# Context turned on VectorE in three pieces, the keys' turn moved one step later, and another order of the last copies and table loads, in a cross-attention kernel

## The chip, the cores and the metric

The kernel runs on one core of a Trainium2 chip. The metric is device time in microseconds (us). Before the change three runs took 446.92, 447.15 and 447.34 us; the median is 447.15 us. The profile comes from one further execution.

## The reference, cut to what matters

Eight batches, each with 112 query rows of 320 channels and a context of 375 rows of 512: 371 text tokens and 4 prompt tokens. There are 20 heads of 16 channels, all in float32.

```python
q   = heads(hidden_states @ W_q)
k_t = heads(text_ehs @ W_k);  v_t = heads(text_ehs @ W_v)
probs_t  = softmax(einsum('bhsd,bhtd->bhst', q, k_t) * attn_scale)
text_out = einsum('bhst,bhtd->bhsd', probs_t, v_t)
k_ip = heads(ip_ehs @ W_k_ip);  v_ip = heads(ip_ehs @ W_v_ip)
qsem = l2norm(einsum('bhst,bte->bhse', probs_t, text_ehs))
sem  = einsum('bhse,bne->bhsn', qsem, l2norm(ip_ehs))
fused = einsum('bhsd,bhnd->bhsn', q, k_ip) * attn_scale + 0.5 * sem
ip_out = einsum('bhsn,bhnd->bhsd', softmax(fused) * spatial_mask, v_ip)
out = (text_out + ip_out) @ W_out + b_out + hidden_states
```

The length of `qsem` is had without forming it: with the context's own product `G = ctx ctx^T`, its square is `p G p^T` for each row of probabilities `p`. So one wide product of `p` gives the value sums, the dots with the prompts and `p G` at once.

## The kernel before, in words

**Per batch, the context is turned first.** `ct` (128 x 3 x 512) holds 375 rows, 128 to a chunk. `transposed_context(b)` turns each chunk with four TensorE transposes (L357) into a bank of PSUM, and ScalarE copies it (L367) into `ctxT`, with the 512 features on the partitions (4 blocks `e` of 128) and the tokens along the row. From `ctxT` come `gram(b)` (L415), `values(b)` (L486) and `keys(b)` (L453). All three sum over the 512 features; so the order in which features lie on `e` and on the partitions doesn't matter as long as the weights are laid out in the same order (`load_embed`, L114). The last 64 channels of the keys come as extra columns of `values`, are put in `k3`, and are turned by three TensorE transposes (L444): this is the keys' last chunk.

**Heads go in five groups of four.** A step is a pair (b, g). For each step:

- `scores` (L592, PSUM pool `ps_sc` of two banks) and `probabilities` run two steps ahead (`LEAD`): VectorE takes the maximum (L605), ScalarE the exponential (L609), and a DMA from SP's queue copies `p` into `xg` (L614). `ps_sc` also serves other products that ask for a `spare` bank; the rest take one of the two banks of `ps_mm`.
- `transposed` turns a group's `xg` on VectorE (L622), one step ahead, after the third of the twelve parts of the running product.
- `multiplied` is the product (L641): 12 parts of 4 heads, into four banks of PSUM (`ps_qd`, four in all). The next step's product needs those banks again, so they must have been read.
- `value_sums` (ScalarE, L654) and `reduced` (VectorE, L687, four times) read them; after the last read the banks are free.
- `between(b, g)` puts the next batch's preparation on TensorE in this place, while the banks are read: for g = 0 the gram, for 1 two thirds of the values, for 2 the rest of the values and the first chunk of keys, for 3 the second chunk, the turn of the third (L444) and the transposes of the finished batch's attention (L837, `finish`), for 4 the context of batch b + 2 (L357), the output product (L849) and a chunk of queries (L305).

**The order of the work** on TensorE, VectorE and SP is written out by hand and so, after the prologue, is ScalarE's; GpSimd (POOL) is placed by the scheduler until the last batch, and by hand there. SP's one queue issues nearly all DMAs in order, each `xg` copy among them. `load_next(b + 2)` issues the four DMAs of a context at the end of step (b, 0), four steps ahead of its turn at (b, 4).

**The end** (batch 7) has no next batch. After the last product, `finish(b, (0, 16))` treats sixteen heads, `last_heads` the last four, and `finish(6)`, called `before`, is still to be completed. Each needs a square root, then an exponential, and ScalarE loads a table (`preload_act_table`) for each change of function. The statements from `value_sums(b, g)` on (L1180 to L1199) set this order.

Of the kernel before, what the change touches and what calls it, by code (L numbers as in the profile page):

```python
# [8 lines left out]
F32 = mybir.dt.float32  # L9
AF = mybir.ActivationFunctionType  # L10
# [10 lines left out]
def kernel(  # L21
# [15 lines left out]
    P = 128  # L37
# [20 lines left out]

    GROUP = 4
# [54 lines left out]
    def load_embed(eng, t, w):  # L114
        eng.dma_start(t[:, :, :C], w.rearrange("(e p) f -> p e f", p=P))
# [7 lines left out]

    def load_ctx(b):
        ct = io.tile([P, NT, E], F32, tag="ct", name=f"ct_{b}")
        for c in range(NT):
            rows = min(P, T - c * P)
            some = rows - rows % 16
            nc.sync.dma_start(ct[:some, c, :], ehs[b, c * P : c * P + some, :])
            if some < rows:  # L130
                nc.sync.dma_start(ct[some:rows, c, :], ehs[b, c * P + some : c * P + rows, :])
        return ct
# [82 lines left out]
    def normalised_prompts():  # L215

        sq = work.tile([N, E], F32, tag="ipn", name="ipsq", bufs=1)
        ss = small.tile([N, 1], F32, tag="ipss", name="ipss", bufs=1)
        nc.vector.tensor_tensor_reduce(
            out=sq, in0=ip_sb, in1=ip_sb, scale=1.0, scalar=0.0, op0=ALU.mult, op1=ALU.add,  # L220
            accum_out=ss,
        )
        nc.vector.tensor_scalar_max(ss, ss, EPS * EPS)
        rn = small.tile([N, 1], F32, tag="iprn", name="iprn", bufs=1)
        nc.scalar.activation(rn, ss, AF.Sqrt)
        nc.vector.reciprocal(rn, rn)

        ipn = work.tile([N, E], F32, tag="ipn", name="ipn", bufs=1)
        nc.vector.tensor_scalar(ipn, ip_sb, rn, 0.5, op0=ALU.mult, op1=ALU.mult)
        yield  # L230

        for src, dst, n in ((ipn, ipnT, "n"), (ip_sb, ipT, "r")):
            ps = bank(f"ps_ipT{n}")
            for e in range(NE):
                nc.tensor.transpose(
                    ps[:, e * N : (e + 1) * N], src[:, e * P : (e + 1) * P], ident[:N, :N]
                )
            nc.vector.tensor_copy(
                dst, ps[:, : NE * N].rearrange("p (e n) -> p e n", n=N)
            )  # L240
        yield
# [86 lines left out]
    def begin(b):  # L328
        s = st[b] = dict(ct=loaded.pop(b))
        s["ctxT"] = work.tile([P, NE, TP], F32, tag="ctxT", name=f"ctxT_{b}")  # L330
        nc.gpsimd.memset(s["ctxT"][:, :, T:], 0.0)

        s["kT"] = work.tile([P, NC, T], F32, tag="kT", name=f"kT_{b}")
        s["vext"] = work.tile([P, NT, C + REST], F32, tag="vext", name=f"vext_{b}", bufs=1)
# [14 lines left out]
    def transposed_context(b):  # L349
        begin(b)  # L350
        s = st[b]
        ct, ctxT = s["ct"], s["ctxT"]
        for c in range(NT):
            rows = min(P, TT - c * P)
            ps = bank(f"ps_c_{b}_{c}", spare=b > 1 and c > 0)
            for e in range(NE):
                nc.tensor.transpose(  # L357
                    ps[:, e * P : e * P + rows],
                    ct[:rows, c, e * P : (e + 1) * P],
                    ident[:rows, :rows],  # L360
                )
# [72 lines left out]
    def keys(b):  # L434
# [3 lines left out]
        for i in range(NC):  # L438
            ps = bank(f"ps_k_{b}_{i}")
# [39 lines left out]
    def values(b):  # L479
        s = st[b]  # L480
        ctxT, vext = s["ctxT"], s["vext"]
# [222 lines left out]
    def finish(b, heads=(0, H), bd=None):  # L704
# [69 lines left out]
        if bd is not None:  # L774
# [9 lines left out]
            for i in range(i0, i1):  # L784
# [10 lines left out]
                )  # L795
            aT = work.tile([P, NC, S], F32, tag="aT", name=f"aT_{b}_{h0}")
# [84 lines left out]
    def last_heads(b):  # L881
# [9 lines left out]
        def over_ip(t):  # L891
# [16 lines left out]
        nc.scalar.preload_act_table(AF.Exp)  # L908
        yield
# [8 lines left out]
        nc.scalar.activation(ex, fu, AF.Exp)  # L918
        nc.vector.tensor_reduce(sx, ex, AX.X, ALU.add)
        nc.vector.reciprocal(rx, sx)  # L920
        nc.vector.scalar_tensor_tensor(w, ex, sm_sb, over_ip(rx), ALU.mult, ALU.mult)
        yield

        ps = bank(f"ps_a_{b}_{h0}")
        nc.tensor.transpose(ps[:, :S], attn[:, FULL * P :], ident[:S, :S])
        aT = work.tile([P, NC, S], F32, tag="aT", name=f"aT_{b}_{h0}")
        nc.scalar.copy(aT[:, FULL, :], ps[:, :S])
        nc.tensor.matmul(
            s["o"][:S, :C], aT[:, FULL, :], wo_sb[:, FULL, :], start=False, stop=False
        )  # L930
# [6 lines left out]
        nc.scalar.copy(wT[:k], ps[:k, :S])  # L937
        nc.tensor.matmul(s["o"][:S, :C], wT[:k], s["bw"], start=False, stop=True)
# [14 lines left out]
    LEAD = 2  # L953
# [11 lines left out]
    def between(b, g):  # L965
# [26 lines left out]
        if g == 3:  # L992
            if new:
                run(("k", nb), None, 1)
            for bs in first if b > 0 else ():
                run(("q", bs[0]), lambda: project_queries(bs), 3)
            if b == 0:
                run(("t", b), lambda: prompt_logits(b))
            if nb < B - 1:
                run(("k", nb), None, 1)  # L1000
            if b > 0 and new:
                run(("f", b - 1), None)
            for bs in rest:
                run(("q", bs[0]), None)
        if g == 4:
            if nb + 1 < B:
                run(("c", nb + 1), lambda: transposed_context(nb + 1))
            if b > 0 and new:
                run(("f", b - 1), None, 2)
            if nb + 1 < B:  # L1010
                run(("c", nb + 1), None, 2)
# [51 lines left out]
    for n, (b, g) in enumerate(steps[:-NG]):  # L1063
# [27 lines left out]
        if g == 0:  # L1091
            load_next(b + 2)
        elif g == 1:
# [91 lines left out]
    run(before, None)  # L1185
    next(late)
# [3 lines left out]
    nc.scalar.preload_act_table(AF.Sqrt)  # L1190
    run(before, None)
    reduced(b, g, 1)
    next(first)
    last = last_heads(b)
    next(last)
# [47 lines left out]
```

## Time and profile before

| | |
|---|---|
| median of three runs | 447.15 us (446.92 to 447.34) |
| the profiled execution | 447.37 us, span 445.6 us |
| TensorE matmuls busy | 433.7 us (97%) |
| VectorE busy | 306.9 us (69%) |
| ScalarE busy | 197.0 us (44%) |
| GpSimd busy | 111.1 us (25%) |
| packets of SP's DMA queue | 51530, 53.4% of 16 DMA engines' span |
| granted TensorE clock | 0.997 |

The span runs from the first instruction to the last. Busy time counts overlapping instructions once. "PE" is TensorE, "PEld" its weight loads, "DVE" VectorE, "ACT" ScalarE, "POOL" GpSimd, "SPq" the instructions by which SP issues DMAs. An entry "A <- B" of waiting says that A stood idle until B had ended. The chain of waits is followed back from the last instruction to what released it, step by step.

### The profile page before, as it was taken

To read this page: it belongs to the slowest core of one execution; us is meant where nothing else is said; L and a number is where in the kernel's file an instruction comes from. 1 tells how busy PE (TensorE), PEld (TensorE's weight loads), DVE (VectorE), ACT (ScalarE), POOL (GpSimd) and SP (SyncE) were. 2 spreads that over 40 slices of the span, in tenths; PEclk is the share of its full clock that TensorE was granted. 3 is DMA by queue.
4 is the path that set the end of the run, shared out by engine and by line. 5 is a ranking of instruction groups with operands and counts; after the bars stand their busy time and mean duration, and the time that the engine had idled before them with its cause. 6 is when DMAs were issued, how large, how long until landed. Compare 5 with 4: busy or idle time off the path is not lost.

```text
span 445.6 us, 13074 instructions
## 1 busy us (share of the span) xinstructions
PE 433.7 (97%) x5096; PEld 335.3 (75%) x5096; DVE 306.9 (69%) x646; ACT 197.0 (44%) x667; POOL 111.1 (25%) x270
## 2 busy tenths in 40 slices
PE   8998999999999999999999999999999999999895
PEld 8756767888778877788777787788777887787783
DVE  3047366786687767686687866776687867878783
ACT  2254232335345353343534453333535454436773
POOL 4302201011150111511142120612124111527340
PEclk9999999999999999999999999999999999999998
DMA  8769954544645466555646366455556436563300
GB/s 241 188 165 259 202 144 138 142 141 138 171 122 135 144 171 164 130 134 143 164 119 166 113 179 165 120 143 152 155 166 145 140 86 180 134 144 105 92 2 26
DMA packets 52031, 64.26 MB, mean 144 GB/s; under 512 B 18354, under 2 KB 44130, under 8 KB 51970
## 3 DMA queue, kind: packets, MB, share of 16 engines
q1 hardware_dynamic: 51530, 62.88, 53.4%
q8 instruction: 40, 0.66, 0.7%
q10 hardware_dynamic: 440, 0.56, 0.4%
q14 instruction: 21, 0.17, 0.1%
HBM read 18.72 MB, written 5.32 MB: 54 GB/s over the span
## 4 chain that ended last, share of the span: by engine, by line
PE 91%; ACT 3%; DMA 2%; DVE 1%; POOL 1%; SPq 0%; issue 0%; POOLq 0%; DVEq 0%; ACTq 0%
PE ps_qd L641 42%; PE ps_v L486 14%; PE ps_k L453 9%; PE ps_g L415 8%; PE ps_s L592 4%; PE ps_q L305 3%; PE ps_c L357 2%; PE ps_o L849 2%; ACT p L609 1%; PE ps_g L387 1%; DMA vr<-vd 1%; DMA xg<-p 1%; DVE xgT L622 1%; PE ps_k L469 1%; DMA ct<-in_ctx_dram 1%; POOL shared L676 1%
## 5 line engine op out<-in xcount | busy, mean ns | idle before, releaser
L641 PE MATMUL ps_qd<-u,xgT 32*112 32x104 f32 (+11 forms) x3840 | 217.9, 351 | 3.1 <-DVE xgT L622 1.2
L641 PEld LDWEIGHTS ps_qd<-u,xgT 32*112 32x112 f32 x3840 | 185.7, 172 | 36.2 <-issue 9.8
L605 DVE TENSOR_REDUCE nmx<-ps_s 112x1 f32<-112x371 f32 x160 | 77.5, 529 | 72.8 <-PE ps_s L592 72.8
L622 DVE STREAM_TRANSPOSE xgT<-xg 128x1536 f32<-128x1536 f32 x40 | 119.0, 2975 | 7.8 <-DMA xg<-p 7.8
L609 ACT ACTIVATE p<-ps_s,nmx 112x371 f32<-112x371 f32 x160 | 87.0, 583 | 80.6 <-DVE nmx L605 58.4
L687 DVE CUSTOM_DVE_ANT_0 junk<-ps_qd,p 112x371 f32<-112x371 f32 x148 | 80.2, 542 | 15.7 <-ACT pvs L654 0.2
L559 POOL COPY u<-vr 128x64 f32<-128x64 f32 x120 | 25.8, 237 | 162.4 <-PE ps_qd L641 105.6
L592 PE MATMUL ps_s<-kT,qm 32*112 32x375 f32 (+1 forms) x320 | 64.0, 481 | 0.4 <-ACT p L609 0.4
L486 PE MATMUL ps_v<-wv_sb,ctxT 128*128 128x384 f32 (+1 forms) x192 | 63.5, 480 | 0.0
L486 PEld LDWEIGHTS ps_v<-wv_sb,ctxT 128*128 128x128 f32 x192 | 35.2, 190 | 19.7
L453 PE MATMUL ps_k<-ctxT,wk_sb 128*128 128x371 f32 x136 | 45.9, 482 | 0.0
L654 ACT COPY pvs<-ps_qd 112x21 f32<-112x21 f32 x150 | 15.9, 190 | 63.1 <-PE ps_qd L641 63.1
L415 PE MATMUL ps_g<-ctxT 128*128 128x375 f32 (+2 forms) x168 | 37.4, 379 | 0.0
L453 PEld LDWEIGHTS ps_k<-ctxT,wk_sb 128*128 128x128 f32 x136 | 25.1, 190 | 15.3 <-issue 0.5
L415 PEld LDWEIGHTS ps_g<-ctxT 128*128 128x128 f32 x168 | 28.1, 190 | 8.4
L592 PEld LDWEIGHTS ps_s<-kT,qm 32*112 32x112 f32 x320 | 25.6, 170 | 5.8 <-ACT kT L460 2.0
L314 DVE TENSOR_SCALAR qm<-ps_q,emask 128x224 f32<-128x224 f32 (+1 forms) x25 | 9.2, 400 | 21.8 <-PE ps_q L305 21.8
L611 ACT COPY ipl<-ps_s 112x4 f32<-112x4 f32 x140 | 23.6, 169 | 0.0
L493 ACT COPY vext<-ps_v 128x384 f32<-128x384 f32 (+1 forms) x24 | 11.2, 467 | 24.3 <-PE ps_v L486 24.3
L460 ACT COPY kT<-ps_k 128x371 f32<-128x371 f32 x17 | 8.0, 469 | 26.0 <-PE ps_k L453 26.0
L403 ACT ACTIVATE ug<-ps_g 128x375 f32<-128x375 f32 (+2 forms) x24 | 9.0, 377 | 23.0 <-PE ps_g L415 18.7
L824 POOL TENSOR_TENSOR wv<-vip,w 112x1280 f32<-112x1280 f32 x6 | 14.8, 2461 | 14.6 <-DVE w L770 14.6
(158 smaller groups left out, 333.1 us busy)
## 6 DMA issues: line engine op xcount, KB each, us to landing
xg<-p SPq DMA_DIRECT2D x160, 162.3 KB
u<-ug SPq DMA_DIRECT2D x128, 99.0 KB
ct<-in_ctx_dram SPq DMA_DIRECT2D x16, 256.0 KB
vr<-vd SPq DMA_DIRECT2D x32, 120.0 KB
vip<-vipd SPq DMA_DIRECT2D x6, 560.0 KB
vd<-vext SPq DMA_DIRECT2D x7, 320.0 KB
ct<-in_ctx_dram SPq DMA_DIRECT2D x8, 224.0 KB
vd<-vext SPq DMA_DIRECT2D x7, 160.0 KB
```

The costliest lines, as they stand in the source:

```text
L415: nc.tensor.matmul(ps[:, : T - t0], ctxT[:, e, t0 : t0 + P], ctxT[:, e, t0:T], start=(e == 0), stop=(e == NE - 1),)
L453: nc.tensor.matmul(ps[:, :TT], wk_sb[:, e, i * P : (i + 1) * P], s["ctxT"][:, e, :TT], start=(e == 0), stop=(e == NE - 1),)
L486: nc.tensor.matmul(ps[:, :w], ctxT[:, e, c * P : (c + 1) * P], wv_sb[:, e, :w], start=(e == 0), stop=(e == NE - 1),)
L559: nc.gpsimd.tensor_copy(region(b, c)[:, :, UV - c * P :], s["vr"][:, c * QN : (c + 1) * QN, g, :])
L592: nc.tensor.matmul(ps[:S, :w], qm[a * RG : (a + 1) * RG, i, r, j * S : (j + 1) * S], s["kT"][a * RG : (a + 1) * RG, i, :w], start=True, st ...
L605: nc.vector.tensor_reduce(nmx, ps[:S, :TT], AX.X, ALU.max, negate=True)
L609: nc.scalar.activation(p, ps[:S, :TT], AF.Exp, bias=nmx)
L611: nc.scalar.copy(s["ipl"][:, groups[g][a], :], ps[:S, TT:T])
L622: nc.vector.transpose(xT.rearrange("p j (k q) -> p q j k", q=QN), xg.rearrange("p q (j k) -> p q j k", k=RG),)
L641: nc.tensor.matmul(banks[a][:S, j * RG : UW], xT[a * RG : (a + 1) * RG, j, :S], region(b, c)[a * RG : (a + 1) * RG, q, q * RG :], start=(j ...
L654: nc.scalar.copy(s["pvs"][:, h, :], ps[:S, TT:UW])
L687: nc.vector.tensor_tensor_reduce(out=junk, in0=ps[:S, :TT], in1=s["p", g][:, a, :], scale=1.0, scalar=0.0, op0=ALU.mult, op1=ALU.add, accu ...
```

## The change

Batches 0 and 1 are turned as before. For batches 2 to 7:

- the context is loaded in another layout: each 32 tokens x 128 features go to a block of 32 partitions (`v`, 12 columns of 128 features), by eight DMAs in place of four: four of 32 x 11 runs of 128 floats, and four of 19 rows of 128 floats for the rest. A memset on GpSimd clears the last column first;
- three VectorE transposes (32 x 32 blocks, 128 x 512 elements each) write `ctxT` in place of twelve TensorE transposes and three ScalarE copies. They stand one each in `between` for g = 0, 1 and 2 (for batch 0: 1, 2, 3), so that the turn is finished at (b, 2) and no longer at (b, 4); the load is issued at the end of step (b - 1, 4), one step ahead of its first use. Batch 2's is issued at the end of step (0, 0), as before;
- since a partition now holds features `4 p + e`, the weights that multiply `ctxT` are loaded in that order too, and the transposes that remain on TensorE read every fourth feature (`chunk`).

In `between`, the turn of the keys' third chunk (L444) goes from g = 3 to g = 4, into a bank of `ps_sc`; the transposes of the finished batch's attention stand right behind the keys' second chunk. At the end, the table of the square root is loaded ahead of the copies of `aT`, the products of the outputs come after the transposes of the last heads' attention, and the last heads' square root and exponential come ahead of the copy of the sixteen heads' `aT`.

```diff
     def load_embed(eng, t, w):
-        eng.dma_start(t[:, :, :C], w.rearrange("(e p) f -> p e f", p=P))
+        eng.dma_start(t[:, :, :C], w.rearrange("(p e) f -> p e f", e=NE))
+    def chunk(t, e):
+        return t.rearrange("t (p e) -> t e p", e=NE)[:, e, :]
     def load_ctx(b):
         ct = io.tile([P, NT, E], F32, tag="ct", name=f"ct_{b}")
+        if b >= LEAD:
+            v = ct.rearrange("p c e -> p (c e)").rearrange("p (j f) -> p j f", f=P)
+            full = TT // RG
+            nc.gpsimd.memset(v[:, full, :], 0.0)
+            for a in range(QN):
+                nc.sync.dma_start(
+                    v[a * RG : (a + 1) * RG, :full, :],
+                    ehs[b, : full * RG, a * P : (a + 1) * P].rearrange("(j i) f -> i j f", i=RG),
+                )
+            for a in range(QN):
+                nc.sync.dma_start(
+                    v[a * RG : a * RG + TT - full * RG, full, :],
+                    ehs[b, full * RG : TT, a * P : (a + 1) * P],
+                )
+            return v
...
     def begin(b):
-        nc.gpsimd.memset(s["ctxT"][:, :, T:], 0.0)
+        if b < LEAD:
+            nc.gpsimd.memset(s["ctxT"][:, :, T:], 0.0)
...
     def transposed_context(b):
+        if b >= LEAD:
+            for c in range(NT):
+                some = slice(c * QN, (c + 1) * QN)
+                nc.vector.transpose(
+                    ctxT[:, :, c * P : (c + 1) * P].rearrange("p e (j i) -> p j e i", i=RG),
+                    ct[:, some, :].rearrange("p j (k e) -> p j e k", e=NE),
+                )
+                yield
+            return
...
     def keys(b):
-            ps = bank(f"ps_k_{b}_{i}")
+            ps = bank(f"ps_k_{b}_{i}", spare=0 < b < B - 1 and i == FULL)
...
     def between(b, g):
         if g == 3:
             if new:
                 run(("k", nb), None, 1)
+            if b > 0 and new:
+                run(("f", b - 1), None)
...
-        if g == 4:
-            if nb + 1 < B:
-                run(("c", nb + 1), lambda: transposed_context(nb + 1))
-            if b > 0 and new:
-                run(("f", b - 1), None, 2)
-            if nb + 1 < B:
-                run(("c", nb + 1), None, 2)
+        if 0 <= g - (b == 0) < NT and nb + 1 < B:
+            run(("c", nb + 1), lambda: transposed_context(nb + 1))
+        if g == 4:
+            if b > 0 and new:
+                run(("f", b - 1), None, 2)
+            if nb < B - 1:
+                run(("k", nb), None, 1)
...
-        if g == 0:
+        if n == 0:
             load_next(b + 2)
-        elif g == 1:
+        if g == NG - 1:
+            load_next(b + 3)
+        if g == 1:
...
     late = projected_prompts(bd[:, 1])
     run(before, None)
     next(late)
-    run(before, None)
-    next(late)
+    nc.scalar.preload_act_table(AF.Sqrt)
+    run(before, None, 2)
     reduced(b, g, 0, 1)
     next(first)
     next(first)
-    nc.scalar.preload_act_table(AF.Sqrt)
-    run(before, None)
+    next(late)
     reduced(b, g, 1)
     next(first)
     last = last_heads(b)
     next(last)
+    run(before, None)
+    next(last)
+    next(first)
     next(last)
     next(first)
     next(last)
```

`finish` has one more `yield` between the transposes and the copy of `aT`, `last_heads` issues its transpose (L925) right behind the square root and its product (L928) behind the transposed weights' copy, and `vext` is allocated in `values` and no longer in `begin`.

## The prediction

> **What bounds the kernel now.** I read the busy times first, then the chain of waits, then the timeline around one step of kind g = 4, then VectorE's own timeline, and last the end.
>
> ```profile
> PE 433.7 (97%) x5096; PEld 335.3 (75%) x5096; DVE 306.9 (69%) x646; ACT 197.0 (44%) x667; POOL 111.1 (25%) x270
> ...
> PE 91%; ACT 3%; DMA 2%; DVE 1%; POOL 1%; SPq 0%; issue 0%; POOLq 0%; DVEq 0%; ACTq 0%
> ```
>
> TensorE is both the busiest engine and 91% of the chain, so an instruction taken from it in the steady part is worth its own length, if nothing else then ends later. The same chain in order of time, one step of batch 1, g = 4 (start, length, what):
>
> ```profile
> 140.58 1.05 PE ps_qd L641 x41
> 142.22 1.61 PE ps_o L849 x6
> 143.84 0.83 PE ps_c L357 x8
> 144.67 1.15 PE ps_q L305 x6
> 145.82 1.15 PE ps_qd L641 x10
> ```
>
> The product ends at 141.63 and the next begins at 145.82: 4.19 us. In it stand the output product 1.61, the queries 1.15, and the twelve context transposes: 0.83 for eight, and 4.19 - 1.61 - 0.83 - 1.15 = 0.60 for the first four (too short to be listed): 1.43 us a batch. What must be over in such a gap is VectorE's reading of the four banks:
>
> ```profile
> 141.51 0.93 DVE L605 TENSOR_REDUCE nmx<-ps_s 112x1 f32<-112x371 f32 x2
> ...
> 144.45 0.54 DVE L687 CUSTOM_DVE_ANT_0 junk<-ps_qd,p 112x371 f32<-112x371 f32 x1
> ```
>
> The fourth bank is free at 145.0, 3.4 us after the product's end. The next product's first part has four heads in turn and takes 0.76 us to the scores behind it (145.75 to 146.51), so its fourth head comes some 0.57 us after its start: the gap can shrink to about 3.4 - 0.57 = 2.8 us before TensorE waits for VectorE. That is the floor which I hold each gap against.
>
> **The steady part: what is removed and moved.** (1) Twelve transposes go in each of six batches. For b = 1 to 4 the gap at g = 4 becomes 4.19 - 1.43, plus the keys' turn that moves in. That turn is three transposes: at 0.60 / 4 = 0.15 to 0.83 / 8 = 0.10 each, 0.4 us. So 3.2 us, over the floor. At g = 3 the same 0.4 us goes away: 136.27 - 131.95 = 4.3 us becomes 3.9, also over the floor. Moving is worth nothing by itself; the two gaps together give 1.43 us. For b = 5 the queries are half as wide (0.67): 3.70 becomes 2.7, at the floor; I take off 0.1. For b = 0 the gap is 3.4 us with 0.5 us of waiting for ScalarE's copies of the scores, whose banks the second and third chunk take; the keys' turn, now first there, asks for such a bank too and begins no sooner (92.2). Behind it stand 0.4 where 0.94 stood: 0.5, and 0.4 from g = 3, 0.9 us. Attention's transposes ahead of the queries' input in `ps_sc` make the third of those wait for a copy of 0.44 us: 0.1 in three batches. Sum: 4 x 1.43 + 1.33 + 0.9 - 0.3 = 7.65 us.
>
> (2) Eighteen copies of 0.58 us leave ScalarE (L367). It is 44% busy, and no step of the chain above is one: nothing.
>
> (3) Eighteen VectorE transposes come in. No row has this form; the nearest is the turn of `xg`, and with it the slack they must fit in:
>
> ```profile
> L622 DVE STREAM_TRANSPOSE xgT<-xg 128x1536 f32<-128x1536 f32 x40 | 119.0, 2975 | 7.8 <-DMA xg<-p 7.8
> ...
> 157.97 0.99 DVE L605 TENSOR_REDUCE nmx<-ps_s 112x1 f32<-112x371 f32 x2 [2.95 <-PE ps_s L592]
> 168.69 1.00 DVE L605 TENSOR_REDUCE nmx<-ps_s 112x1 f32<-112x371 f32 x2 [3.25 <-PE ps_s L592]
> 179.33 0.99 DVE L605 TENSOR_REDUCE nmx<-ps_s 112x1 f32<-112x371 f32 x2 [1.25 <-PE ps_s L592]
> ```
>
> 2975 ns for 1536 elements to a partition gives 0.99 us for 512. Here it is the read that steps by four floats, there the write; so between 0.5 us (twice the rate) and 2 us (half); I take 1.0. They stand just ahead of the three waits of 2.95, 3.25 and 1.25 us (g = 0, 1, 2), in which VectorE waits for scores: all hidden. At 2 us the third would be late by 0.75, and so would the banks one step on: 2.8 + 0.75 is still under 3.9. It costs nothing at either end. The Trainium skill speaks against this ("VectorE: DVE Perf Modes", Rules for kernel authors): a 128 x 128 transpose belongs on TensorE if PSUM will do as its target. In unit price the trace agrees, 1.43 us a batch on TensorE against some 3.0 on VectorE; if VectorE set the time, the sum would read 6 x 3.0 = 18 us slower. The rows choose: the 1.43 is on the chain, the 3.0 in waits of 7.45.
>
> (4) Loads. A context is 371 rows x 4 pieces = 1,484 packets of 512 B where 375 of 2 KB went, and is issued one step ahead of its use. SP's packets now take 0.534 x 445.6 x 16 / 51530 = 74 ns on average; 1,484 over 16 engines make 6.9 us, at half that price (they are smaller than the average, 1,220 B) 3.4. Issued at 144.4 behind the `xg` copies, eight issues at about 0.5 us, then 3 us to land as in the chain's `xg<-p` of 3.04: in place between 151 and 155. VectorE wants the first piece at 155.0 (behind its reads and two short operations of `finish`); 1.95 us are left in that wait and 1.9 more in the gap at g = 1 (5.36 us, less the 3.4): a load may land as late as 158.9 without cost. Behind the eight in SP's queue come the prompts' values (needed a batch later) and two `xg` copies, ready at 148.5 and now issued about a microsecond later; they are read by the turn at 158.9. The six context loads leave g = 0, where they stood behind the same kind of copies. Nothing, up to some 2 us a batch if `xg` is held. GpSimd's memset of a column has a row of similar size at 0.2 us and is issued a batch ahead of its load; the copy of the prompts' features (L410) now waits for VectorE's third piece, but that is behind the weights `w` in both engines' order, and GpSimd is 25% busy: nothing.
>
> (5) Prologue. The transposes left on TensorE read with a step; bound 0 to 12 x 0.11 = 1.3 us for batch 0 (batch 1's lie under the 1.16 us that TensorE waits for `u`); I take 0. `W_v` in longer runs: its consumer ends at 11.0 and TensorE needs it at 13.0: nothing.
>
> **The end.** ScalarE's timeline:
>
> ```profile
> 432.44 0.17 ACT L868 COPY bT<-ps_bT 64x16 f32<-64x16 f32 x1
> 434.00 0.44 ACT L797 COPY aT<-ps_a 128x336 f32<-128x336 f32 x1 [1.40 <-PE ps_a L789]
> ...
> 435.21 1.28 ACT L1190 ACT_TABLE_LOAD   x1
> 437.94 0.35 ACT L797 COPY aT<-ps_a 128x224 f32<-128x224 f32 x1 [1.45 <-PE ps_a L789]
> 438.19 0.21 ACT L907 ACTIVATE rn_last<-rn_last 112x4 f32<-112x4 f32 x1
> 438.41 1.28 ACT L908 ACT_TABLE_LOAD   x1
> 439.71 0.22 ACT L918 ACTIVATE ex_last<-fu_last 112x16 f32<-112x16 f32 x1
> ```
>
> The square root is ready to go at 435.4 (VectorE's last input ends at 435.34) and goes at 438.19, behind a copy that waits for TensorE; the exponential's table and all behind it are late by that. After: the first load fits the 1.40 us wait at 432.6; copies end at 435.4; square root 435.4, table to 436.8, exponential 436.9, `aT` 437.3, weights `w` 437.6. TensorE then has no more waits: from 431.96, by the rows of the chain, 0.43 + 1.55 (transposes) + 0.22 + 0.64 + 0.9 to 1.43 + 0.21 + 1.62 + 1.1 to 1.2 + 0.2, and two products of 0.54 and 0.8: 440.2 to 440.9, plus up to 0.2 for the waits that I can't see. Before it was 442.19: a gain of 1.1 to 2.0, I take 1.4. A rule against it: the Trainium skill ("ScalarE: Activation LUTs", What ACT_TABLE_LOAD costs) gives 1.28 us for a load and 1.38 us of draining, 2.66 for every switch. The row shows 1.28, and the exponential 0.02 us behind it. By the rule the load at 432.6 would end at 435.3, hold the copies by 1.3, the second would end at 439.2, and the last product come at some 442: no gain, 440.6 rather than the sum below. I go by the row.
>
> **The sum.** 7.65 + 1.4 = 9.05 us. The profiled execution, 447.37 (445.6 of span and 1.77 around it), becomes 438.3; the median shown is 0.22 lower: 438.1 us.
>
> **Rivals.**
> A. VectorE becomes the limit in the short gaps: the floor of 2.8 is not reached but say 3.4 (the banks must all be free before the product can begin at all), or the bank for the keys' turn isn't free. Then g = 4 saves 0.8 in place of 1.0 for b = 1 to 4, nothing for b = 0, 0.3 for b = 5, and a piece that is slower than 1.25 in g = 2 pushes g = 3. With all of it some 3 us are lost: 441. For it: the turn of `xg` ends at 141.67 and VectorE has no wait until the banks are read. Against: the waits of 7.45 us a batch.
> B. The load lands late, slower than before. Its place is VectorE's first piece, in order ahead of the maxima, which feed all. From 158.9 each microsecond costs one in each of the five batches loaded one step ahead. It cancels the gain at 158.9 + 9.05 / 5 = 160.7, 16 us after issue, which takes 150 ns for a packet, twice the mean; at 162, 3.1 x 5 = 15.5 us are lost: 453.6. For it: DMA engines are half busy already and other copies share them. Against: the mean price of a packet, though 44,130 of the 52,031 are under 2 KB already.
> C. The end gives nothing (the drain, or copies that wait) and the prologue's stepping reads cost 0.5: 440.
> D. TensorE's removal isn't paid in full as its waits come back elsewhere, e.g. through held `xg` copies (0.9 us a batch, 5.4 in all): 443.5. Against: three microseconds between landing and use. No case has the change do nothing: the transposes do leave TensorE.
>
> **How the numbers follow.** The forecast 0.56, A 0.15, B 0.09, C 0.12, D 0.05, no change within 0.2% (losses that happen to match) 0.03. 0.2% of 447.15 is 0.9 us, about what a measurement tells from no change. Faster 0.56 + 0.15 + 0.12 + 0.05 = 0.88; same 0.03; slower 0.09. The range reaches from the full gain (6 x 1.43 + 2.0 = 10.6, 436.6) to A with a part of C and D, 442.6; B and the worst of D stay outside.
>
> **What would show it.** Right: no `ps_c` behind the prologue; gaps at g = 4 of 3.2 us and at g = 3 of 3.9; eighteen transposes near 1.0 us; no wait of VectorE for `ct`; the waits ahead of the maxima shorter by 1.0; the square root at 3.5 us after the last product's end and not 6.2. Wrong: a wait "VectorE <- DMA ct" or "TensorE <- VectorE" in the gaps, pieces over 2 us, `xg` landing after its turn is due.

## The result: half of the forecast gain, and the profile after

The changed kernel takes 442.56 us (median of 4 runs, 442.2 to 444.0) where the kernel before takes 447.25 (4 runs): a ratio of 0.9895, 95% interval 0.988 to 0.991. A second set of 6 runs gives 443.22 us and 0.9896 (0.9863 to 0.9928). The forecast was 438.1 us, a gain of 9.05 us; 4.7 came. The range that was stated, 436.6 to 442.6 us, holds the first median by 0.04 us and not the second: with this scatter that is luck. The profiled execution takes 444.0 us, 442.3 of them span.

The page of the kernel after: the busy times, then the shares of the chain that ended last, then two groups (busy us, mean ns of one, idle time before them).

```profile
PE 429.4 (97%) x5024; PEld 330.7 (75%) x5024; DVE 325.5 (74%) x664; ACT 189.0 (43%) x649; POOL 111.7 (25%) x270
...
PE 88%; ACT 3%; DMA 3%; DVE 3%; issue 1%; POOL 1%; SPq 0%; POOLq 0%; DVEq 0%
...
L654 DVE STREAM_TRANSPOSE xgT<-xg 128x1536 f32<-128x1536 f32 x40 | 119.1, 2979 | 12.1 <-DMA xg<-p 8.2
...
L378 DVE STREAM_TRANSPOSE ctxT<-ct 128x512 f32<-128x512 f32 x18 | 19.8, 1103 | 0.1
```

TensorE's 72 instructions are gone and VectorE has 19.8 us more, in pieces of 1.10 us that wait for nothing (0.1 us in all). But the chain is 88% TensorE, not 91%: 3% of the span moved to VectorE and DMA. The same chain in order of time, over steps g = 3 and g = 4 of batch 1 (start, length, what):

```profile
132.38 1.05 PE ps_qd L673 x41
133.43 2.71 PE ps_k L484 x8
...
137.40 1.15 PE ps_qd L673 x10
...
141.71 1.05 PE ps_qd L673 x41
142.77 1.80 PE ps_o L883 x6
144.57 0.32 PE ps_k L475 x3
144.88 1.15 PE ps_q L326 x6
146.03 1.15 PE ps_qd L673 x10
147.18 0.23 PE ps_s L624 x2
147.41 0.08 PE ps_qd L673 x2
147.48 0.24 PE ps_s L624 x2
...
151.60 1.14 PE ps_g L446 x3
```

The gap at g = 4 is 146.03 - 142.77 = 3.26 us, and the one at g = 3 is 137.40 - 133.43 = 3.97: what the forecast had (3.2 and 3.9). (From the end of the last matmul to the start of the next product's first, which the chain counts 0.07 us later, they are 3.20 and 3.90; before, 4.11 and 4.25. Gaps below are counted so.) The product behind g = 4's gap is what it did not have: 151.60 - 146.03 = 5.57 us where it took 151.19 - 145.82 = 5.37 before. The scores in it stand with 0.23 and 0.24 us on the chain; in the undelayed products of both kernels it is 0.03 and 0.04.

VectorE's timeline of the same kernel: the last of the four banks behind the gap, and the pieces and maxima of the next batch.

```profile
145.58 0.54 DVE L719 CUSTOM_DVE_ANT_0 junk<-ps_qd,p 112x371 f32<-112x371 f32 x1
146.05 0.08 DVE L719 DVE_READ_ACCUMULATOR2_ANT ss<- 112x1 f32 x1
...
155.11 1.12 DVE L378 STREAM_TRANSPOSE ctxT<-ct 128x512 f32<-128x512 f32 x1
158.39 0.99 DVE L637 TENSOR_REDUCE nmx<-ps_s 112x1 f32<-112x371 f32 x2 [2.16 <-PE ps_s L624]
...
165.77 1.09 DVE L378 STREAM_TRANSPOSE ctxT<-ct 128x512 f32<-128x512 f32 x1
169.11 1.00 DVE L637 TENSOR_REDUCE nmx<-ps_s 112x1 f32<-112x371 f32 x2 [2.25 <-PE ps_s L624]
...
178.75 1.10 DVE L378 STREAM_TRANSPOSE ctxT<-ct 128x512 f32<-128x512 f32 x1
179.78 0.96 DVE L637 TENSOR_REDUCE nmx<-ps_s 112x1 f32<-112x371 f32 x2
```

The fourth bank is free at 146.13, 3.36 us after the product's end, as before (3.37). The waits of 2.95, 3.25 and 1.25 us are now 2.16, 2.25 and none: the first two pieces are covered, the third just so.

From the starts of the products in TensorE's timeline (a product starts with its first `ps_qd` matmul behind other work) the whole span can be laid out step by step. A row runs from the start of the product of the step named to the start of the next one. It holds that product and the gap behind it. What the gap at g = 4 does to the product behind it is therefore in the next batch's row g = 0. A batch's "three rows" are its g = 3 and g = 4 and the next one's g = 0.

| row of TensorE, us | before | after | loads spread | keys' turn back |
|---|---|---|---|---|
| batch 1, g = 3 | 9.68 | 9.33 | 9.33 | 9.66 |
| batch 1, g = 4 | 9.55 | 8.63 | 8.63 | 8.30 |
| batch 2, g = 0 | 10.63 | 10.84 | 10.85 | 11.17 |
| batch 0, its three rows | 29.89 | 30.26 | 29.78 | 30.12 |
| batch 4, its three | 30.20 | 29.95 | 29.31 | 29.53 |
| batch 5, its three | 29.22 | 29.02 | 29.92 | 29.54 |

(The last two columns are experiments, below.) Rows g = 1 and g = 2 do not change: 10.73 and 10.63 us before, 10.72 and 10.64 after. Against the prediction's sum, in the profiled executions:

| term | forecast, us | measured, us |
|---|---|---|
| start to the first product | 0 | +1.1 |
| batch 0 | -0.9 | +0.4 |
| batches 1 to 3 (-1.06, -1.23, -1.00) | -4.3 | -3.3 |
| batch 4 | -1.4 | -0.25 |
| batch 5 | -1.3 | -0.2 |
| late `xg` copy in batch 6 | 0 | +0.3 |
| attention's transposes | +0.3 | in the rows above |
| from the start of batch 6, g = 3, to the end | -1.4 | -1.4 |
| sum | -9.05 | -3.3 |

The measured sum is the difference of the spans, 442.3 - 445.6. The medians differ by 4.7. The start is most of that difference, and it is scatter between executions: the first product starts at 36.1 us in the profile before, at 37.2 in that after, at 36.1 to 37.3 in the other profiles (38.4 in one, where the granted clock was 0.90 and 0.76 from 25 to 35 us), and at 37.0 in one whose prologue is that of the kernel before. The last row isn't all of one piece either: behind the last product's end the kernel takes 12.52 us in place of 13.68, which is -1.2; -0.6 is batch 7's first product, which a late `xg` copy had held in the execution before (10.36 us; 9.85 and 9.87 in two others with the same code there); +0.3 is a late turn of `xg` in batch 7.

The end of the kernel after, ScalarE's timeline:

```profile
430.79 1.28 ACT L1218 ACT_TABLE_LOAD   x1
432.18 0.44 ACT L831 COPY aT<-ps_a 128x336 f32<-128x336 f32 x1
...
433.55 0.21 ACT L941 ACTIVATE rn_last<-rn_last 112x4 f32<-112x4 f32 x1 [0.22 <-DVE rn_last L932]
433.77 1.28 ACT L942 ACT_TABLE_LOAD   x1
435.06 0.22 ACT L954 ACTIVATE ex_last<-fu_last 112x16 f32<-112x16 f32 x1
```

The square root goes 0.22 us behind its input and no longer behind a copy. The copy follows the first table load 0.11 us after its end, the exponential the second after 0.01.

### The profile page after: what moved, and what is told of

It is laid out like the page before. It is cut to its first block, busy times and chain, and to the rows that moved or that the text cites. A ratio compares the mean times of both kernels' runs of the same rounds, so it can differ in the third digit from the quotient of the medians.

```text
span 442.3 us, 12958 instructions
## 1 busy us (share of the span) xinstructions
PE 429.4 (97%) x5024; PEld 330.7 (75%) x5024; DVE 325.5 (74%) x664; ACT 189.0 (43%) x649; POOL 111.7 (25%) x270
## 4 chain that ended last, share of the span: by engine, by line
PE 88%; ACT 3%; DMA 3%; DVE 3%; issue 1%; POOL 1%; SPq 0%; POOLq 0%; DVEq 0%
PE ps_qd L673 39%; PE ps_v L518 14%; PE ps_k L484 10%; PE ps_g L446 8%; PE ps_s L624 4%; PE ps_q L326 3%; DMA xg<-p 2%; PE ps_o L883 2%; PE ps_g L418 1%; DVE xgT L654 1%; PE ps_c L388 1%; ACT p L641 1%; PE ps_k L500 1%; DMA ct<-in_ctx_dram 1%; POOL shared L708 1%
## 5 line engine op out<-in xcount | busy, mean ns | idle before, releaser
L673 PE MATMUL ps_qd<-u,xgT 32*112 32x72 f32 (+11 forms) x3840 | 220.5, 353 | 3.2 <-DVE xgT L654 1.3
L624 PE MATMUL ps_s<-kT,qm 32*112 32x375 f32 (+1 forms) x320 | 67.8, 484 | 0.4 <-ACT p L641 0.4
L624 PEld LDWEIGHTS ps_s<-kT,qm 32*112 32x112 f32 x320 | 27.1, 170 | 6.3 <-ACT kT L491 2.1
L378 DVE STREAM_TRANSPOSE ctxT<-ct 128x512 f32<-128x512 f32 x18 | 19.8, 1103 | 0.1
```

The costliest lines, as they stand in the source:

```text
L378: nc.vector.transpose(ctxT[:, :, c * P : (c + 1) * P].rearrange("p e (j i) -> p j e i", i=RG), ct[:, some, :].rearrange("p j (k e) -> p j ...
L624: nc.tensor.matmul(ps[:S, :w], qm[a * RG : (a + 1) * RG, i, r, j * S : (j + 1) * S], s["kT"][a * RG : (a + 1) * RG, i, :w], start=True, st ...
L673: nc.tensor.matmul(banks[a][:S, j * RG : UW], xT[a * RG : (a + 1) * RG, j, :S], region(b, c)[a * RG : (a + 1) * RG, q, q * RG :], start=(j ...
```

## The experiments

Two theories stand against each other for the missing 4.4 us. A: VectorE's reading of the four banks is a floor of some 3.4 us, not 2.8, so part of what leaves the gap at g = 4 comes back in the product behind it. D: the `xg` copies come late, because of the contexts' smaller packets or because VectorE is late. (Where a median is held against the changed kernel's, that is the 443.22 us of its second set.)

### The changed kernel again

No edit; it stands beside the next three.

> The changed kernel, unaltered, for a second profile and a better time. 442.5 us (ratio 0.990). If VectorE's lateness in the short gaps is the cause of the missing half, the gaps at g = 4 and the product behind them stand as in the first profile: 3.3 us, then 5.6 us in place of 5.4. If single DMAs that land late are the cause, the places differ: the 0.9 us at (4, 3) and the 2.5 us at (6, 0) by which the turn of xg waited go, and others come.

443.22 us, ratio 0.9896. Batches 1 to 3 take 50.16, 50.33 and 50.17 us between their first Gram matmuls (50.16, 50.33 and 50.23 in the first profile), so what is gained and lost there is no chance. Batch 0 takes 59.9 us in place of 58.8. That is not the change's doing either; the last section says why. Batch 5's three rows take 31.31 us where they took 29.02: there single executions differ by more than the effect.

### The end alone

```diff
 # kernel before with the change's whole order of the end; three of its lines
+    nc.scalar.preload_act_table(AF.Sqrt)   # ahead of the aT copies
+    ps = bank(f"ps_a_{b}_{h0}")            # last transposes ahead of the wait
+    nc.tensor.transpose(ps[:, :S], attn[:, FULL * P :], ident[:S, :S])
```

> The kernel before with the new order of the end alone. My sum: 1.4 us less, 445.8 (span from the last product's end to the last instruction 12.3 where 13.7 stood). By the rule of a drain behind every table load: no change, 447.2.

446.22 us (12 runs), ratio 0.9963 (0.9947 to 0.9979): 1.6 us faster than the kernel before. The forecast of 1.4 lies within the interval (0.9 to 2.4 us). The prediction's other reading, which left no gain, is refuted for this place.

### The weights' and features' order alone

```diff
-        eng.dma_start(t[:, :, :C], w.rearrange("(e p) f -> p e f", p=P))
+        eng.dma_start(t[:, :, :C], w.rearrange("(p e) f -> p e f", e=NE))
...
-                    ct[:rows, c, e * P : (e + 1) * P],
+                    chunk(ct[:, c, :], e)[:rows],   # every fourth feature
```

> The kernel before with one part of the change alone: weights in the order 4 p + e, and TensorE's transposes of all eight batches reading every fourth feature. If reading with a step is what makes the start 1.1 us later, a transpose costs some 0.1 us more wherever it stands: 1.1 us at the start and up to 12 x 0.1 = 1.2 in each of the batches 2 to 7, so 447.2 + 1.1 + 7.2 = 455 (less where a gap hides it). If the start is late for the weights' loads or by chance, 447 to 448.3.

449.54 us (12 runs), ratio 1.0036 (1.0015 to 1.0057): 1.7 us slower, with all eight contexts turned by TensorE from stepping reads. TensorE's weight loads of the kernel before and of this one, shape by shape:

```profile
L357 PEld LDWEIGHTS ps_c<-ident,ct 128*128 128x128 f32 x64 | 7.7, 147 | 3.1 <-ACT ipl L611 0.7 <-DMA ct<-in_ctx_dram 0.4 <-ACT kT L460 0.4
```

```profile
L360 PEld LDWEIGHTS ps_c<-ident,ct 128*128 128x128 f32 x64 | 9.7, 208 | 2.6 <-ACT ipl L614 0.6 <-DMA ct<-in_ctx_dram 0.4 <-ACT kT L463 0.3
```

A load of stationary operands that steps by four floats takes 208 ns, not 147. The gap at g = 4 is longer by 0.2 us in batches 1 to 5 (4.31 in place of 4.11 in batch 1): 0.02 us a transpose, not the 0.1 of the first view. That is 1.1 us over the batches; where the rest of the 1.7 lies isn't shown. In the changed kernel only batches 0 and 1 are turned so, which puts its price at about 0.4 us by these rows, a quarter of 1.7.

### The keys' third turn back at g = 3

```diff
-            ps = bank(f"ps_k_{b}_{i}", spare=0 < b < B - 1 and i == FULL)
+            ps = bank(f"ps_k_{b}_{i}")
...
-                run(("k", nb), None, 1)     # in g == 4
+                run(("k", nb), None, 1)     # in g == 3
```

> The changed kernel with the turn of the keys' third chunk back at g = 3 and in its former bank. If the bank of the scores is what holds TensorE at (0, 4) (1.65 us) the wait goes and batch 0 is 1 us or more shorter, with g = 3 longer by 0.4 in six batches: some 442.5 - 1.2 + 2.4 - (0.3 at each g = 4, where VectorE sets 3.4) = 442.5 to 443.5. If VectorE, late at (0, 4), is the cause, the product there begins no sooner (95.4), only the name of the wait changes, and the move is worth its 0.4 at each g = 3: 444.5.

444.97 us, ratio 0.9929 (0.9904 to 0.9954): by the medians 1.7 us slower than the changed kernel beside it, but the two intervals overlap, so the rows must decide. Row g = 3 grows by 0.33 us in batches 1 and 3, which is the turn's own time, and by 0.53 in batches 2 and 4, where the queries also wait 0.2 us. Row g = 4 and the next row g = 0 together do not get shorter for it: 8.63 + 10.84 = 19.47 in the changed kernel, 8.30 + 11.17 = 19.47 here. The gap shrinks to 2.87 us and the product behind it grows by the same 0.33. TensorE's weight loads and VectorE's timeline at that place:

```profile
145.96 0.28 PEld L673 LDWEIGHTS ps_qd<-u,xgT 32*112 32x112 f32 x6 [0.28 <-issue]
146.52 0.17 PEld L673 LDWEIGHTS ps_qd<-u,xgT 32*112 32x112 f32 x1 [0.28 <-DVE ss L719]
```

```profile
145.91 0.54 DVE L719 CUSTOM_DVE_ANT_0 junk<-ps_qd,p 112x371 f32<-112x371 f32 x1
146.38 0.08 DVE L719 DVE_READ_ACCUMULATOR2_ANT ss<- 112x1 f32 x1
```

The six loads are those of three heads (two each). The fourth head's waits 0.28 us for `ss`, VectorE's reading of the fourth bank, which ends at 146.46. The changed kernel has the same wait in a shorter form. These are the matmuls of the product that are under way in its first 0.1 us, in the kernel before (from 145.75) and in the changed one (from 145.96), and then the changed one's in its first 0.24 us:

```profile
145.75 0.60 PE L641 MATMUL ps_qd<-u,xgT 32*112 32x392 f32 x4
```

```profile
145.96 0.59 PE L673 MATMUL ps_qd<-u,xgT 32*112 32x392 f32 x3
```

```profile
145.96 0.80 PE L673 MATMUL ps_qd<-u,xgT 32*112 32x392 f32 x4
```

Where no bank is missing, all four heads begin at once (within 0.02 us in the trace). In the changed kernel the fourth begins 0.22 us after the first (0.80 less the 0.58 that one takes), 0.05 behind the end of VectorE's reading at 146.13. So there is a floor. The gap, and what the row behind it has over its usual 10.64 us, add up to it:

| gap at g = 4 of | gap, us | product longer by | sum |
|---|---|---|---|
| before, batch 0 | 3.30 | 0.11 | 3.41 |
| after, batch 1 | 3.20 | 0.20 | 3.40 |
| keys' turn back, batch 1 | 2.87 | 0.53 | 3.40 |
| keys' turn back, batch 0 | 1.47 | 2.01 | 3.48 |
| loads spread, batch 0 | 2.78 | 0.70 | 3.48 |
| transfer moved (below), batch 5 | 2.71 | 0.68 | 3.39 |

Whatever leaves this gap below 3.4 us is given back at once. This is theory A, in batches 1 to 3 and, where VectorE is in time, in batches 0 and 5. For batch 0 this run was to tell whether the scores' bank held the keys' turn there. With the turn gone the product does begin 1.3 us sooner than in the changed kernel's profile (93.98 against 95.29) and gains nothing by it: its weight loads then wait for VectorE bank by bank.

### The pieces earlier

```diff
-        if 0 <= g - (b == 0) < NT and nb + 1 < B:
-            run(("c", nb + 1), lambda: transposed_context(nb + 1))
+        if 0 <= g - (b == 0) < NT - 1 and nb + 1 < B:
+            run(("c", nb + 1), lambda: transposed_context(nb + 1), NT - 1 - g + (b == 0))
```

> The changed kernel with two of VectorE's three pieces in the first step that has one and the third in the second, none in the step after. If the third piece is what makes VectorE late in batch 0 ahead of the gap at g = 4 (TensorE idle for 1.65 us ahead of the keys' turn there), some 1.2 us come back: 441.4. If that wait is the late xg copy (it landed after 4.1 us in the profiled execution), the time stays within 0.5 us of the changed kernel. In batches 1 to 3 both theories expect no change: the first step's wait of 1.9 us takes a second piece of 1.1.

443.38 us, ratio 0.9911 (0.9886 to 0.9935): no faster. Batch 0's rows shrink from 30.26 to 29.56 (8.13 in place of 8.82 in row g = 4). But in four runs below that leave the third piece where it was, and change the loads alone, they take 29.77 to 29.79: 0.2 us is the third piece, and 0.5 the late `xg` copy of the changed kernel's profile. Batches 1 to 3 do not move. What batch 0 gained, batch 5 lost in this execution (30.54 against 29.02), behind a turn of `xg` that waited 1.7 us. So the third piece isn't the main loss.

### The pieces twice

```diff
-                nc.vector.transpose(
+                for _ in range(2):
+                    nc.vector.transpose(
```

> The changed kernel with each of VectorE's eighteen pieces done twice, to the same place: it prices VectorE's time in these three steps. By the prediction's slack (waits of 2.95, 3.25 and 1.25 us, a floor of 2.8 us in the gaps) 1.1 us more in each step costs nothing in g = 0 and 1, and in g = 2 makes the third piece late by 0.9, still under the gap of 3.9: no change, within 0.5 us. With the floor at 3.4 us, 3.4 + 0.9 is 0.4 over the gap of 3.9: 0.4 in each of six batches, and 1.1 more in batch 0, where VectorE is late already: 2 to 3.5 us slower than the changed kernel, 444.5 to 446. If VectorE's time binds in full, 18 x 1.1 = 20 us slower.

448.0 us (12 runs), ratio 1.0008 (0.9995 to 1.0022): 4.8 us slower than the changed kernel, above the 2 to 3.5 that the floor gave. The group and VectorE's timeline in a step with the third piece (batch 2, g = 3):

```profile
L379 DVE STREAM_TRANSPOSE ctxT<-ct 128x512 f32<-128x512 f32 x36 | 39.8, 1105 | 0.7
```

```profile
180.59 2.26 DVE L379 STREAM_TRANSPOSE ctxT<-ct 128x512 f32<-128x512 f32 x2
182.77 0.50 DVE L638 TENSOR_REDUCE nmx<-ps_s 112x1 f32<-112x371 f32 x1
```

20 us more of VectorE cost 4.8, nearly all of it by the third piece, which lies under the product of g = 3: that row is longer by 0.57 to 0.68 us in batches 1 to 5, batch 0's rows g = 3 and g = 4 by 1.1 and 0.65. It isn't the floor that does it in batches 1 to 5. The gaps at g = 3 and the rows g = 4 stay as they were, and the four heads begin together; what is longer is the product of g = 3 itself, in its second half. The maxima come 0.8 us later in the step, so ScalarE's exponentials do, and the two banks of `ps_sc` are free later for the next scores, which go one by one where they went two by two. TensorE's scores there, in the changed kernel (3.6 to 4.4 us after the product's start) and with the pieces twice (3.6 to 5.0):

```profile
181.74 0.50 PE L624 MATMUL ps_s<-kT,qm 32*112 32x375 f32 x2
...
182.07 0.48 PE L624 MATMUL ps_s<-kT,qm 32*112 32x375 f32 x2
```

```profile
183.98 0.56 PE L625 MATMUL ps_s<-kT,qm 32*112 32x375 f32 x1
...
184.91 0.47 PE L625 MATMUL ps_s<-kT,qm 32*112 32x375 f32 x1
```

Rows g = 1 and g = 2, with a doubled piece under each product, stay at 10.72 and 10.64. So two pieces have at least 1.1 us of cover left, and the third has none.

### The loads twice, and in large packets

```diff
+            for a in range(QN):
+                nc.sync.dma_start(extra[a * RG : (a + 1) * RG, :, :], ...)   # same source again
```

> The changed kernel with the four large transfers of each context (1,472 packets of 512 B) issued a second time, to a tile that nobody reads: it prices the smaller packets and SP's queue. If the DMA side is what took 2 to 3 us of the expected gain (theory D), as many transfers more cost about as much again: 444.5 to 446, with VectorE waiting for xg. If VectorE's floor took it, the time is that of the changed kernel within 0.7 us, as three microseconds lie between a copy's landing and its use.

453.72 us (4 runs), ratio 1.0144 (1.0123 to 1.0164): 10.5 us slower, far outside both expectations. The turn of `xg` in the page:

```profile
L660 DVE STREAM_TRANSPOSE xgT<-xg 128x1536 f32<-128x1536 f32 x40 | 119.0, 2976 | 28.1 <-DMA xg<-p 24.6
```

VectorE waits 24.6 us for `xg` where it waited 8.2. Row g = 2 takes 1.4 to 2.0 us longer in batches 1 to 5. The opposite edit takes the small packets away:

```diff
-            for a in range(QN):            # 4 + 4 transfers, 512 B packets
-                nc.sync.dma_start(v[a * RG : (a + 1) * RG, :full, :], ...)
+            nc.sync.dma_start(ct[:, :n, :], ehs[b, : n * P, :].rearrange("(c p) e -> p c e", p=P))
+            nc.sync.dma_start(ct[: TT - n * P, n, :], ehs[b, n * P : TT, :])
```

> The changed kernel with each context from the third on loaded by rows of 2 KB (371 packets in two transfers) in place of 1,484 packets of 512 B in eight, at the same point; VectorE's pieces and all else stay, but the data lie in another order, so contexts 2 to 7 are scrambled and the output with them. It takes away the DMA price of the change and keeps its VectorE price. If the small packets took what is missing (4.4 us between the forecast's sum and the measured time), 439 to 441; if VectorE's reading of the banks took most of it, 442 to 443.

443.26 us, ratio 0.9901 (0.9883 to 0.9919): the time of the changed kernel. Its page:

```profile
q1 hardware_dynamic: 50534, 62.83, 55.7%
...
L649 DVE STREAM_TRANSPOSE xgT<-xg 128x1536 f32<-128x1536 f32 x40 | 119.0, 2976 | 11.5 <-DMA xg<-p 10.5
```

7,000 packets fewer, and the waits for `xg` are not shorter. As placed, the loads cost nothing that these runs can tell, which is to one or two microseconds. As many again cost 10.5 us: the slack behind them is real, and less than twice the load.

### The loads at other places

```diff
-        if g == NG - 1:
+        if g == 1:          # first version
+        if g == 0:          # second version
             load_next(b + 3)
```

> The changed kernel with the loads of each next context issued behind g = 1 rather than behind g = 4, so that their eight transfers no longer stand in SP's queue ahead of the xg copies of a batch's first steps. Theory D (xg copies held or slowed by these loads and their neighbours): VectorE's turns of xg that waited for their copy near 89, 288 and 353 us wait no more, and 1 to 3 us come back: 440 to 441.5. Theory A alone (the missing gain is the floor in the gap at g = 4, set by VectorE): the steps of batches 1 to 3 stay at 50.2 us and the time is that of the changed kernel within 0.5 us. A third view: any late copy is chance, its place shifts, and the time stays the same with the waits at other places.

448.14 us (12 runs), ratio 1.0007 (0.9988 to 1.0027): behind g = 1 the whole gain is lost, against each of the three views. VectorE's timeline, batch 1:

```profile
133.56 2.97 DVE L654 STREAM_TRANSPOSE xgT<-xg 128x1536 f32<-128x1536 f32 x1 [2.52 <-DMA xg<-p]
```

The eight transfers stand there in SP's queue with the values' way to DRAM, ahead of the `xg` copies that the turn in g = 3 reads; SP takes 3.4 us to issue the eight. Batch 1's row g = 3 takes 10.66 us in place of 9.33.

> The changed kernel with each next context's loads behind g = 0, where the kernel before had them, rather than behind g = 4, where a transfer of 560 KB (the prompts' values) goes as well. If what costs time is that the two stand together (the DMA engines full for some 12 us at each batch's turn, the xg copies behind them late), the late copies of batches 0, 4 and 5 go and 1 to 2.5 us come back: 441 to 442. If the packets cost the same wherever xg copies follow them (as they did behind g = 1, where the time rose by 5 us), 443 to 447.

443.54 us, ratio 0.9913 (0.9889 to 0.9936): behind g = 0, the time of the changed kernel. The eight transfers in three parts, four behind g = 0 and two each behind g = 2 and g = 3:

```diff
+    SPREAD = {0: 2, 2: 1, 3: 1}
...
+        if g in SPREAD:
+            load_next(b + 3, SPREAD[g])
```

> The changed kernel with the eight transfers of each next context spread over steps: four behind g = 0, two behind g = 2 and two behind g = 3. No xg copy then stands behind more than two large transfers. If it is the length of the queue ahead of a copy that makes it late, this is the fastest of all: 440 to 441.5, and VectorE waits for xg no longer than in the kernel before. If the sum of packets counts and not their place, the time is that of the changed kernel, within 0.7 us.

442.46 us (442.32 to 443.3), ratio 0.9893 (0.9874 to 0.9911): the time of the changed kernel, not the 440 to 441.5 of the first view. Batch 0's row is 29.78 and batch 4's 29.31 in its profile, better by 0.5 and 0.6; batch 5's is 29.92. There VectorE and SP's queue show this:

```profile
332.79 2.97 DVE L659 STREAM_TRANSPOSE xgT<-xg 128x1536 f32<-128x1536 f32 x1 [1.57 <-DMA xg<-p]
```

```profile
SPq L651 <- DMA vipx<-vipd: 1.2, 1, 1.2
```

The second pair of `xg` copies was issued 1.2 us late, behind one transfer of 200 KB from DRAM to DRAM that both kernels make in batch 5. The kernel before has the same wait (1.1 us) and, with its longer batch, room for it; the changed kernel's profile has it with 0.8 us.

### That transfer one step earlier

```diff
-        if (b, g) == (B - 3, 1):
+        if (b, g) == (B - 3, 0):
             prompt_values_by_head()
```

> The kernel with spread loads, and the one transfer of the last two batches' prompt values from DRAM to DRAM (200 KB) one step earlier, behind batch 5's g = 0 rather than its g = 1. In batch 5 SP's queue waited 1.2 us on that transfer ahead of the second pair of xg copies, and VectorE's turn of xg waited 1.6 us for its copy; the batch took 51.3 us where the forecast's steps give 49.3. If that wait is what batch 5 lost, 1 to 2 us come back: 440.5 to 441.5, with no wait of VectorE near 333 us. If VectorE is late there by its own added pieces, or another transfer takes its place, the time stays at that of the spread loads (442.5), within 0.5 us.

442.08 us (440.71 to 444.24), ratio 0.987 (0.9847 to 0.9893). In the profile the wait near 333 us is gone and batch 5's rows take 9.24 + 8.15 + 11.31 = 28.70 us, 1.2 less than with spread loads and less than in each of the ten profiles of the changed kernel and its variants that have the transfer in its old place (29.02 to 31.31). So the transfer is what cost batch 5 its time with spread loads. What is left there, 28.70 against 29.22 before, is 0.5 of the 1.3 us that were forecast: the rest is the floor (2.71 + 0.68 in the table above). In the medians the 0.4 us between the two kernels can't be told from their scatter. This is the best of the kernels run, and 442.08 is not measurably better than the changed kernel's 442.56.

## Why the forecast was half right

**Where the missing part is.** The profiled execution falls 5.7 us short of the forecast's sum. By the rows some 2.2 are the floor (0.6 in batch 0, 0.2 in each of batches 1 to 4, 0.8 in batch 5), 0.2 the third piece in batch 0, 2.1 late turns of `xg` (0.5, 1.0, 0.3 and 0.3 in batches 0, 4, 5 and 6), and 1.1 the start, which is scatter.

**Steady part, -7.65 forecast (step 1).** The mechanism was right, and both gaps came out as worked. The step that failed is the floor of 2.8 us: "its fourth head comes some 0.57 us after its start". The four heads don't go in turn: in the kernel before, all four begin within 0.02 us, so nothing is to be taken off the 3.4 us at which the fourth bank is free, and gap plus stretch measures 3.40 to 3.48. The lines shown in the prediction don't tell this; the start of the product, head by head, does. This is rival A, given 0.15, and its figures came nearly one by one: g = 4 with the row behind it saves 0.7 us in batches 1 to 3 (0.8 was said), nothing in batch 0, 0.24 in batch 5 with the transfer moved (0.3). Only its reason is too strong: the product can begin before all banks are free, but its fourth head can't.

**"Moving is worth nothing by itself".** Wrong for the same reason. The keys' turn left a gap that was above the floor and went into one that would have lain below it. It is worth 0.33 us (0.53 in batches 2 and 4) in each of batches 0 to 4, 2.0 us by the rows and 1.7 by the medians, over half of the 3.1 us (4.7 - 1.6) that all but the end gave.

**Batch 0, -0.9 forecast.** +0.4 came. Its gap at g = 4 stood at the floor already in the kernel before (3.30 + 0.11), so the 0.5 forecast there could not come; 0.3 came at g = 3. 0.2 is lost to the third piece. The other 0.5 is an `xg` copy of 4.11 us from issue to landing. It is missing with the loads spread, doubled or in large packets, and with the keys' turn back, which changes nothing at that place: it isn't shown to be the loads' doing, and what held it stays open. The keys' turn began at 93.67 and not at 92.2, behind that turn of `xg`.

**Batches 4 and 5, -2.8 forecast, -0.45 measured.** The floor, and rival D's waits, given 0.05, but not from its source. In batch 5 they come from the DRAM-to-DRAM transfer. In batch 4 SP issued the `xg` copies late, behind four `u` issues of which one took 2065 ns, where the median is 588. SP's timeline, and then the answer for this line alone (durations in ns: minimum, median, maximum):

```profile
283.27 3.96 SPq L460 DMA_DIRECT2D u<-ug  x4
```

```profile
L460 SPq DMA_DIRECT2D u<-ug x4: 582/588/2065, 283.3 to 286.6; - x4
```

The four take 2.48 us elsewhere. Groups of four slower than 2.7 us stand in batches 4 and 5 of every profile with the change, large packets among them. In the kernel before slow ones stand at other places. What holds them stays open, and no run took them away; so does the part of batch 4's loss that is left with spread loads (29.31 us, where batch 2's same rows take 28.97).

**VectorE's pieces, cost 0 (step 3).** The price was 1.10 us for a forecast of 1.0, and each was covered as the waits said, in batches 1 to 4. "At 2 us the third would be late by 0.75" and free was wrong: doubled to 2.26, it costs 0.6 us a batch. The prediction followed the lateness to the four banks only; it reaches TensorE sooner, by the scores' two banks. The rule of the Trainium skill weighed there ("VectorE: DVE Perf Modes", Rules for kernel authors: a 128 x 128 transpose belongs on TensorE if PSUM will do as its target) did not decide here: the first 19.8 us on VectorE were nearly free, the second 19.8 cost 4.8.

**Loads, cost 0 (step 4).** Right as placed, by the large packets. The bound of "2 us a batch if `xg` is held" is of the size of what happens behind g = 1 or with doubled loads (4.9 / 6 = 0.8 and 10.5 / 6 = 1.75 us a load).

**End, -1.4.** Right: behind the last product's end -1.2 in the profile and -1.1 in that of the end alone, -1.6 in the latter's medians. The square root goes 3.8 us after the last product's end (forecast 3.5).

**Prologue, 0 (step 5).** The stepping reads' 0.4 us, an estimate from the rows of batches 1 to 4, lie within the bound of 0 to 1.3; the 0 taken was low.

**The signs named.** No `ps_c` behind the prologue, both gaps, the eighteen pieces, no wait for `ct`, the square root: all seen. The waits ahead of the maxima are shorter by 0.8, 1.0 and 1.25. What was named as wrong, "`xg` landing after its turn is due", was seen in batches 0, 4, 5 and 6, and "TensorE <- VectorE" is the wait at the floor.

## What to carry to other kernels

When a gap on the busiest engine is made shorter, hold it and the work behind it together against what frees that work's buffers: here gap plus stretch was 3.4 to 3.5 us, whatever was taken out. Read from the trace, head by head, how much of the next work can begin before the last buffer is free. Work that is moved between two such gaps is worth its time if it leaves the one above the floor. And slack is not to be read from a steady batch alone: the terms that failed most were batches 0, 4 and 5, where a gap stood at the floor already, or a single late issue or transfer had used the slack up.

## What the hardware showed beside this

The granted TensorE clock drops for some 10 us in four of the fourteen profiled executions: from 25 to 35 us in one, between 45 and 57 us in two, from 91 to 101 us in one. The windows of the profiled execution with the transfer moved (stretch, length, busy us and count of PE, PEld, DVE, ACT and POOL, then the granted clock, DMA share and GB/s):

```profile
47.00:52.00 5.00, 5.00 (x37) 3.88 (x36) 2.37 (x7) 1.21 (x5) 2.23 (x6) 0.85 1.00 223
52.00:57.00 5.00, 5.00 (x42) 2.69 (x44) 1.02 (x3) 0.81 (x2) 0.34 (x2) 0.81 0.85 161
```

The first product's row took 17.20 us there, 17.19 in the other execution with a drop at that place (the loads behind g = 1; 0.94 and 0.72 from 45 to 55 us), and 15.50 in all others. In the repeated changed kernel it fell on 91 to 101 us (0.80 and 0.86): there the queries' six matmuls behind batch 0 take 2.24 us in place of 1.31, which is most of that batch's 1.1 us. Of that kernel's six runs the two with a mean clock of 0.996 and below took 445.9 and 446.4 us, the other four 442.2 to 443.3. A difference of one microsecond between two single profiles is therefore no finding here before the step rows show where it lies.
